# Feed-forward activations with a token's chunks side by side, and one convolution tap of every second chunk moved from VectorE to ScalarE and GpSimd

## The chip, the core and the metric

The kernel runs on one core of a Trainium2 chip. A core has a matrix engine (TensorE, PE in the profile, with its weight loads as PEld), a vector engine (VectorE, DVE), a scalar engine for activations (ScalarE, ACT), a general engine (GpSimd, POOL), and a queue engine that issues most of the transfers (SP). The engines run side by side, each through its own queue in program order, and wait for one another by semaphores. The metric is the device time of the program in microseconds (us), as the median of several runs.

## What is computed

A cross-attention layer followed by a quantized feed-forward layer, each with a residual, for one sequence of 2048 tokens of 256 features and a context of 1601 tokens. The change lies in the feed-forward layer:

```python
def act_quant(x):
    scale = 127.0 / jnp.clip(jnp.max(jnp.abs(x), axis=-1, keepdims=True), 1e-05)
    return jnp.clip(jnp.round(x * scale), -128, 127) / scale
...
h = bit_linear(x, w1)                                        # 256 -> 1024, inputs and weights quantized
h = depthwise_conv1d(h.transpose(0, 2, 1), conv_w, conv_b)   # three taps along the tokens
h = h.transpose(0, 2, 1)
h = jax.nn.silu(h)
return bit_linear(h, w2)                                     # 1024 -> 256, inputs and weights quantized
...
x = x + _L0_xattn_ref(ctx_1024, _layernorm(x, axis=-1), mask_BxS2_bk0, ...)
x = x + _L0_ffn_ref(_layernorm(x, axis=-1), L0_ffn_w1, L0_ffn_conv_w, L0_ffn_conv_b, L0_ffn_w2)
```

The depthwise convolution has for each of the 1024 hidden features its own three weights and a bias: output token t is made of the hidden tokens t-1, t and t+1. The second `bit_linear` quantizes each token's 1024 activations with one scale, which needs the largest magnitude over all of them.

## The kernel before

The attention part comes first: keys and values from the context and the tokens, then eight units (four blocks of 512 query tokens by two pairs of heads), then the output projection, the residual and the quantization of the feed-forward layer's inputs, block of 128 tokens by block. This part ends at about 855 us, but its last four blocks are finished in between the work of the feed-forward part: `plan` holds the calls with the step at which each is due.

The feed-forward part works with features on the 128 partitions and tokens along the free axis. The 1024 hidden features are `NH = 8` chunks of 128. The tokens are taken in 8 groups (`NG`) of `G = 256`. The work is cut into 32 slots: slot s handles group `s // 4` and the pair of chunks `2 * (s % 4)` and the next one (`NP = 4` pairs to a group). `slot(s)` (line 935) writes out the order of the instructions; each engine keeps the program's order, since `tensor`, `vector`, `scalar` and `gpsimd` there are wrappers that forbid reordering (`InOrder`, line 157; the profile puts all of their instructions on line 165, so they are told apart by the names of their tiles). For one pair of chunks the stages are

- `hidden` (line 820): four matmuls with `w1T` into `ph`, 256 tokens and one neighbour on each side, in one of two PSUM buffers. It is called at the end of the slot before.
- `dequantize` (831): DVE multiplies `ph` by the tokens' units `ib_all` into `h`, both chunks in one instruction.
- `taps` (840): ACT makes of `h` the middle tap with the bias, in `t`, and the first tap, in `side`; four instructions of 128x256.
- `last_tap` (854), one slot later: DVE adds the third tap to `t`, one instruction for each chunk; then POOL adds `t` to `side`, both chunks in one instruction.
- `silu` (864), two slots later: ACT puts the Silu of `side` into `t`.

`t` is laid out by chunk and then by token, `[P, NH, G]`. When the four pairs of a group are done, `later_pieces` (928) places, by slots after the group's first:

- 6: `magnitudes` (868), the largest magnitude over the 8 chunks, one DVE reduction of 2048 elements into `m`;
- 7: `columns` and `scales` (875, 881): PE transposes `m`, DVE reduces it over the partitions into `am2` and makes the scale `qsc`; POOL fills `cm` with the scale along rows;
- 8: `scales_spread` (889): PE transposes `cm` into `tpb`, so that each token's scale stands on all partitions; then `rounding(g, 0)`;
- 9: `rounding(g, 1)` (894): DVE multiplies half of `t` (four chunks, all tokens) by the scales and rounds it into `hq`, by adding and taking away a large constant;
- 10: `product` (908): for each of two blocks of 128 tokens eight matmuls, with `hq` as the weights and `w2T` moving, into `py`;
- 11: `residual_out` (918): DVE scales `py`, adds the residual, and SP stores it.

Inside a slot the order is `silu(s-2)`, `dequantize(s)`, `taps(s)`, in slots 3, 7, ... the units of a later group (`unit_rows`, with two `cm` fills on POOL), `last_tap(s-1)`, then the later pieces, and `hidden(s+1)` at the end. So in a slot where a product is due, PE takes the product before the next `ph`.

Of the kernel before, what the change touches and what calls it, by code (L numbers as in the profile page):

```python
# [9 lines left out]
F32 = mybir.dt.float32  # L10
BF16 = mybir.dt.bfloat16
U8 = mybir.dt.uint8
AF = mybir.ActivationFunctionType
ALU = mybir.AluOpType
AX = mybir.AxisListType
PSUM = bass.MemoryType.PSUM

P = 128
FMAX = 3.4028234663852886e38
MAGIC = 12582912.0  # L20
# [6 lines left out]
def kernel(  # L27
# [30 lines left out]
    NH = HID // P  # L58
    NQB = NL // P
    G = 256  # L60
# [45 lines left out]
    w2T = const.tile([P, NH, D], BF16, name="w2T")  # L106
    cw_sb = const.tile([P, NH, 3], F32, name="cw_sb")
# [61 lines left out]
    tensor, vector = InOrder(nc.tensor), InOrder(nc.vector)  # L169
    scalar, gpsimd = InOrder(nc.scalar), InOrder(nc.gpsimd)  # L170
# [36 lines left out]
    with tc.tile_pool(name="pro", bufs=1, side="right") as pro, tc.tile_pool(  # L207
        name="pw", bufs=2, side="right"
# [238 lines left out]
    with att:  # L447
# [297 lines left out]
        for k, (u, j) in enumerate(steps):  # L745
            i = k % NKB
            g, pr = units[u]
# [46 lines left out]
    fp = ctx.enter_context(tc.tile_pool(name="fp", bufs=2))  # L794
# [8 lines left out]
    NP = NH // 2  # L803
    groups_ = [{} for _ in range(NG)]
    chunk = {}
# [32 lines left out]
        chunk[s]["h"] = h  # L838

    def taps(s):  # L840
        g, c = s // NP, s % NP * 2
        if c == 0:
            groups_[g]["t"] = fp.tile([P, NH, G], F32, tag="t", name="t", bufs=3)
        t, h = groups_[g]["t"], chunk[s]["h"]
        side = fp.tile([P, 2, G], F32, tag="side", name="side", bufs=3)
        for j in range(2):
            scalar.activation(
                t[:, c + j, :], h[:, j, 1 : G + 1], AF.Identity,
                bias=cb_sb[:, c + j : c + j + 1], scale=cw_sb[:, c + j, 1:2],
            )  # L850
            scalar.activation(side[:, j, :], h[:, j, 0:G], AF.Copy, scale=cw_sb[:, c + j, 0:1])
        chunk[s]["side"] = side

    def last_tap(s):
        g, c = s // NP, s % NP * 2
        t, h, side = groups_[g]["t"], chunk[s]["h"], chunk[s]["side"]
        for j in range(2):
            vector.scalar_tensor_tensor(
                t[:, c + j, :], h[:, j, 2 : G + 2], cw_sb[:, c + j, 2:3], t[:, c + j, :],
                ALU.mult, ALU.add,  # L860
            )
        gpsimd.tensor_tensor(side, side, t[:, c : c + 2, :], ALU.add)

    def silu(s):
        g, c = s // NP, s % NP * 2
        scalar.activation(groups_[g]["t"][:, c : c + 2, :], chunk.pop(s)["side"], AF.Silu)

    def magnitudes(g):
        b = groups_[g]
        b["m"] = fp.tile([P, G], F32, tag="m", name="m")  # L870
        vector.tensor_reduce(
            b["m"], b["t"].rearrange("p c t -> p t c"), AX.X, ALU.max, apply_absolute_value=True
        )

    def columns(g):
        b = groups_[g]
# [14 lines left out]
        b["tb"] = small("tpb")  # L891
        repeat_rows(b["tb"], b.pop("cm"))

    def rounding(g, c):
        b = groups_[g]
        half = b["t"][:, ts(c, NH // 2), :]
        vector.tensor_tensor(
            half, half,
            b["tb"].rearrange("p i t -> p (i t)").unsqueeze(1).to_broadcast([P, NH // 2, G]),
            ALU.mult,  # L900
        )
        if c == 0:
            b["hq"] = fp.tile([P, NH, G], BF16, tag="hq", name="hq")
        vector.tensor_scalar(
            b["hq"][:, ts(c, NH // 2), :], half, MAGIC, -MAGIC, ALU.add, ALU.add
        )

    def product(g):
        b = groups_[g]
        b["py"] = ps_y.tile([P, QPG, D], F32, tag="py", name="py")  # L910
        for i in range(QPG):
            for c in range(NH):
                tensor.matmul(
                    b["py"][:, i, :], b["hq"][:, c, ts(i, P)], w2T[:, c, :],
                    start=(c == 0), stop=(c == NH - 1),
                )

    def residual_out(g):
# [8 lines left out]

    later_pieces = {
        6: (magnitudes,), 7: (columns, scales),
        8: (scales_spread, lambda g: rounding(g, 0)), 9: (lambda g: rounding(g, 1),),  # L930
        10: (product,), 11: (residual_out,),
    }
    last = NG * NP

    def slot(s):
        if s == 0:
            unit_spread(0)
            unit_spread(1)
            hidden(0)
        if 0 <= s - 2 < last:  # L940
            silu(s - 2)
        if s < last:
            dequantize(s)
            taps(s)
        if s % NP == 3 and s // NP + 2 < NG:
            unit_rows(s // NP + 2)
        if 0 <= s - 1 < last:
            last_tap(s - 1)
        for g in range(NG):
            for call in later_pieces.get(s - g * NP, ()):  # L950
                call(g)
            if g > 1 and s == (g - 2) * NP + 3:
                unit_spread(g)
        if s + 1 < last:
            hidden(s + 1)
# [41 lines left out]
```

## Time and profile before

| | |
|---|---|
| median of 3 runs | 1016.02 us (1014.09 to 1018.25) |
| time of the profiled execution | 1019.8 us, of which the span is 1018.0 us |
| feed-forward part | from about 855 us to the end of the span |
| TensorE clock granted over the span, mean | 0.899; in windows of the feed-forward part 0.56 to 0.63 |
| ACT, taps into `t` and into `side`, 128x256 | 64 each, 0.591 and 0.493 us in the mean |
| ACT, Silu, 128x512 | 32, 0.628 us |
| DVE, third tap, 128x256 | 64, 0.528 us in the mean, 0.476 in the median |
| DVE, maximum over the chunks, 2048 elements to 256 | 8, 3.660 us |
| POOL, `side` plus `t`, 128x512 | 32, 1.270 us |
| PE, product matmuls and their weight loads | 128, 0.421 and 0.151 us in the median |

The profile is of one execution; the sum of the costs is compared with that execution's own time. Instructions of one engine overlap at their ends, so the distance from one start to the next is often somewhat shorter than the duration. A line of the timeline or of the table of groups names the engine, the kernel's line, the operation, the tile written and the tiles read, the shapes, the count, and in the end the idle time of the engine before it with what ended it. In the chain of waits each line is the start, the length, the engine and the tile of one stretch.

### The profile page before, as it was taken

What the parts mean: (1) busy time and instruction counts of PE and PEld (TensorE: products, weight loads), DVE (VectorE), ACT (ScalarE), POOL (GpSimd) and SP (SyncE); (2) the same over time, 40 slices, a digit from 0 to 9 for tenths busy, and PEclk for the clock granted to TensorE, in tenths of its full rate; (3) what the DMA queues carried; (4) which work ended last, traced back from release to release, by engine and by line L of the source; (5) the groups of instructions that cost most, each with busy time, mean ns of one, the idle gap of its engine ahead of it and who ended that gap; (6) DMA issues with size and microseconds to landing.
All of it is one profiled execution on the core that took longest, in us unless ns stands there. A gap on an engine that the chain in (4) does not pass through costs nothing.

```text
span 1018.0 us, 10253 instructions
## 1 busy us (share of the span) xinstructions
PE 859.8 (84%) x3672; PEld 323.7 (32%) x3672; DVE 819.0 (80%) x946; ACT 523.0 (51%) x706; POOL 537.6 (53%) x415
## 2 busy tenths in 40 slices
PE   4788978998998999899899999989998877555543
PEld 3334532222322333232233323223332323333321
DVE  4566447996898689779868998977898995799996
ACT  2456444554654644455454566556554435755560
POOL 2432343556555556646655675646566546545431
PEclk9999998999999999899989999999998897556565
DMA  5010002453444344245534335544344000000000
GB/s 133 21 33 10 1 0 58 87 104 80 86 91 97 83 83 82 62 84 99 109 75 79 75 83 104 96 92 98 69 84 102 22 0 21 1 11 11 21 10 32
DMA packets 29775, 63.28 MB, mean 62 GB/s; under 512 B 7259, under 2 KB 16668, under 8 KB 29724
## 3 DMA queue, kind: packets, MB, share of 16 engines
q0 software_dynamic: 14112, 51.39, 25.8%
q1 hardware_dynamic: 12030, 10.44, 3.3%
q10 hardware_dynamic: 3582, 0.79, 0.4%
q8 instruction: 29, 0.48, 0.2%
q14 instruction: 22, 0.18, 0.1%
HBM read 9.13 MB, written 2.10 MB: 11 GB/s over the span
## 4 chain that ended last, share of the span: by engine, by line
PE 53%; DVE 36%; ACT 5%; issue 2%; POOL 2%; DMA 2%; ACTq 0%; POOLq 0%; DVEq 0%
PE sa L165 15%; PE ot L165 15%; PE st L165 10%; DVE mxs L165 6%; DVE sg L165 5%; PE kv L353 5%; DVE t L165 4%; DVE m L165 3%; PE sa L179 3%; DVE acd L165 2%; DVE y L165 2%; DVE h L165 2%; DVE hi L165 1%; DVE rows L165 1%; DVE hq L165 1%
## 5 line engine op out<-in xcount | busy, mean ns | idle before, releaser
L165 POOL TENSOR_TENSOR acc<-acc,pt 128x1024 f32<-128x1024 f32 x112 | 283.2, 2529 | 36.0 <-ACT pt L165 35.5
L165 PE MATMUL ot<-pt,v_sb 128*64 128x512 f32 x928 | 254.2, 633 | 2.0 <-ACT pt L165 1.9
L165 DVE TENSOR_TENSOR sg<-sg,nb 128x1024 f32<-128x1024 f32 x104 | 218.2, 2104 | 14.1 <-ACT nb L165 14.1
L165 PE MATMUL sa<-q_un,kT 64*128 64x512 f32 x812 | 223.9, 640 | 3.0 <-DVE mxs L165 3.0
L165 POOL DMA_DIRECT2D acd<-pt x98 | 84.0, 857 | 214.6 <-ACT pt L165 156.9
L165 ACT ACTIVATE sg<-sa,maskc 128x1024 f32<-128x1024 f32 x91 | 101.2, 1112 | 177.1 <-PE sa L165 176.9
L165 ACT ACTIVATE pt<-st 128x1024 f32<-128x1024 f32 x128 | 130.9, 1023 | 77.4 <-PE st L165 77.3
L165 DVE TRANSPOSE_TENSOR_REDUCE mxs<-sa 128x32 f32<-128x1024 f32 x112 | 137.2, 1231 | 34.4 <-PE sa L165 33.6
L165 DVE TRANSPOSE_TENSOR_REDUCE mxs<-sg 128x32 f32<-128x1024 f32 x91 | 112.7, 1238 | 40.8 <-ACT sg L165 40.8
L165 PE MATMUL st<-q_un,kT 64*128 64x512 f32 x512 | 141.8, 633 | 0.0
L165 ACT ACTIVATE pt<-sg 128x1024 f32<-128x1024 f32 x104 | 109.3, 1051 | 41.9 <-DVE sg L165 41.9
L165 PEld LDWEIGHTS sa<-q_un,kT 64*128 64x128 f32 x812 | 64.0, 186 | 138.7 <-issue 88.3
L165 PEld LDWEIGHTS ot<-pt,v_sb 128*64 128x64 f32 x928 | 48.8, 139 | 183.8 <-issue 174.1
L165 POOL TENSOR_TENSOR side<-side,t 128x512 f32<-128x512 f32 x32 | 40.6, 1270 | 48.8 <-DVE t L165 47.8
L165 PEld LDWEIGHTS st<-q_un,kT 64*128 64x128 f32 x512 | 53.4, 202 | 34.9 <-issue 31.1
L165 ACT ACTIVATE t<-h,cb_sb,cw_sb 128x256 f32<-128x256 f32 x64 | 37.9, 591 | 38.6 <-DVE h L165 38.6
L353 PE MATMUL kv<-wkv_sb,feat 128*128 128x512 f32 (+1 forms) x116 | 55.5, 620 | 0.0
L165 PE MATMUL st<-rows,ones 64*128 64x512 bf16 x256 | 52.4, 403 | 1.5 <-DVE mxs L165 1.5
L329 DVE TENSOR_TENSOR nn<-raw,ss 128x512 f32<-128x512 f32 (+1 forms) x23 | 15.7, 681 | 47.0 <-POOL ss L101 47.0
L165 PE MATMUL py<-w2T,hq 128*128 128x256 bf16 x128 | 30.2, 417 | 26.4 <-DVE hq L165 26.4
L101 POOL TENSOR_TENSOR ss<-ss,neg_half 128x8 f32<-128x8 f32 (+1 forms) x23 | 37.7, 1638 | 1.9
L97 POOL TENSOR_SCALAR ss<-ss 128x8 f32<-128x8 f32 (+1 forms) x23 | 5.8, 253 | 60.2 <-DVE ss L320 60.1
(130 smaller groups left out, 1001.1 us busy)
## 6 DMA issues: line engine op xcount, KB each, us to landing
acd<-pt POOLq DMA_DIRECT2D x98, 512.0 KB, 4.5
tok<-in_x_dram SPq DMA_DIRECT2D x4, 512.0 KB, 3.5
q_un<-in_x_dram SPq DMA_DIRECT2D x4, 512.0 KB, 3.6
w_sb<-in_L_ffn_w_dram SPq DMA_DIRECT2D x4, 512.0 KB, 3.2
out_dram<-res SPq DMA_DIRECT2D x16, 128.0 KB, 1.8
tok<-in_ctx_dram SPq DMA_DIRECT2D x3, 512.0 KB, 4.1
wkv_sb<-in_L_xattn_W_kv_dram ACTq DMA_DIRECT2D x1, 512.0 KB, 9.0
wo_sb<-in_L_xattn_W_out_dram SPq DMA_DIRECT2D x1, 256.0 KB, 8.8
```

Of the source, the lines that this page charges most:

```text
L97: gpsimd.tensor_scalar(x, x, floor, None, op)
L101: gpsimd.tensor_tensor(x, x, e, ALU.pow)
L165: return tc.keep_in_program_order(getattr(self.engine, name)(*args, **kwargs))
L179: tensor.matmul(st[:, hh, :], kT[halves(hh), pr, ts(j, P)], qT[g][halves(hh), pr, :], start=start, stop=True,)
L329: nc.vector.tensor_tensor(nn[:rows, :nb, :].rearrange("p b (h d) -> p b h d", d=DH), raw[:rows, :nb, :].rearrange("p b (h d) -> p b h d", ...
L353: nc.tensor.matmul(kv[:rows, b, :], feat[:, c, c0 + b * rows : c0 + (b + 1) * rows], wkv_sb[:, c, :], start=(c == 0), stop=(c == ND - 1),)
```

## The change

The sum of the taps is made in new tiles `pre` and `side`, and `t` holds only the result of the Silu, by token and then by chunk, `[P, G, NH]`. ACT's `taps` gets a fifth instruction, the third tap of the second chunk of the pair, in `side[:, 2]`. `last_tap` has one DVE instruction, for the first chunk, instead of two; POOL adds `side[:, 2]` to `side[:, 1]` first (128x256), and then `side` to `pre` (128x512, as before). `silu` writes its two chunks with a step of 8 elements. `magnitudes` reads neighbours. `rounding` takes 128 tokens with all chunks, rather than four chunks with all tokens, and `hq` is by token and then by chunk too, so that the product's weights are read with a step of 8 elements.

```diff
     def taps(s):
-        g, c = s // NP, s % NP * 2
-        if c == 0:
-            groups_[g]["t"] = fp.tile([P, NH, G], F32, tag="t", name="t", bufs=3)
-        t, h = groups_[g]["t"], chunk[s]["h"]
-        side = fp.tile([P, 2, G], F32, tag="side", name="side", bufs=3)
+        c = s % NP * 2
+        h = chunk[s]["h"]
+        pre = fp.tile([P, 2, G], F32, tag="pre", name="pre", bufs=3)
+        side = fp.tile([P, 3, G], F32, tag="side", name="side", bufs=2)
         for j in range(2):
             scalar.activation(
-                t[:, c + j, :], h[:, j, 1 : G + 1], AF.Identity,
+                pre[:, j, :], h[:, j, 1 : G + 1], AF.Identity,
                 bias=cb_sb[:, c + j : c + j + 1], scale=cw_sb[:, c + j, 1:2],
             )
             scalar.activation(side[:, j, :], h[:, j, 0:G], AF.Copy, scale=cw_sb[:, c + j, 0:1])
-        chunk[s]["side"] = side
+        scalar.activation(side[:, 2, :], h[:, 1, 2 : G + 2], AF.Copy, scale=cw_sb[:, c + 1, 2:3])
+        chunk[s].update(pre=pre, side=side)
 
     def last_tap(s):
-        g, c = s // NP, s % NP * 2
-        t, h, side = groups_[g]["t"], chunk[s]["h"], chunk[s]["side"]
-        for j in range(2):
-            vector.scalar_tensor_tensor(
-                t[:, c + j, :], h[:, j, 2 : G + 2], cw_sb[:, c + j, 2:3], t[:, c + j, :],
-                ALU.mult, ALU.add,
-            )
-        gpsimd.tensor_tensor(side, side, t[:, c : c + 2, :], ALU.add)
+        c = s % NP * 2
+        h, pre, side = chunk[s]["h"], chunk[s]["pre"], chunk[s]["side"]
+        gpsimd.tensor_tensor(side[:, 1, :], side[:, 1, :], side[:, 2, :], ALU.add)
+        vector.scalar_tensor_tensor(
+            pre[:, 0, :], h[:, 0, 2 : G + 2], cw_sb[:, c, 2:3], pre[:, 0, :], ALU.mult, ALU.add
+        )
+        gpsimd.tensor_tensor(pre, pre, side[:, 0:2, :], ALU.add)
 
     def silu(s):
         g, c = s // NP, s % NP * 2
-        scalar.activation(groups_[g]["t"][:, c : c + 2, :], chunk.pop(s)["side"], AF.Silu)
+        if c == 0:
+            groups_[g]["t"] = fp.tile([P, G, NH], F32, tag="t", name="t", bufs=3)
+        t = groups_[g]["t"][:, :, c : c + 2]
+        scalar.activation(t.rearrange("p t c -> p c t"), chunk.pop(s)["pre"], AF.Silu)
 
     def magnitudes(g):
...
-        vector.tensor_reduce(
-            b["m"], b["t"].rearrange("p c t -> p t c"), AX.X, ALU.max, apply_absolute_value=True
-        )
+        vector.tensor_reduce(b["m"], b["t"], AX.X, ALU.max, apply_absolute_value=True)
...
-    def rounding(g, c):
+    def rounding(g, i):
         b = groups_[g]
-        half = b["t"][:, ts(c, NH // 2), :]
+        part = b["t"][:, ts(i, P), :]
         vector.tensor_tensor(
-            half, half,
-            b["tb"].rearrange("p i t -> p (i t)").unsqueeze(1).to_broadcast([P, NH // 2, G]),
-            ALU.mult,
+            part, part, b["tb"][:, i, :].unsqueeze(2).to_broadcast([P, P, NH]), ALU.mult
         )
-        if c == 0:
-            b["hq"] = fp.tile([P, NH, G], BF16, tag="hq", name="hq")
-        vector.tensor_scalar(
-            b["hq"][:, ts(c, NH // 2), :], half, MAGIC, -MAGIC, ALU.add, ALU.add
-        )
+        if i == 0:
+            b["hq"] = fp.tile([P, G, NH], BF16, tag="hq", name="hq")
+        vector.tensor_scalar(b["hq"][:, ts(i, P), :], part, MAGIC, -MAGIC, ALU.add, ALU.add)
 
     def product(g):
...
-                    b["py"][:, i, :], b["hq"][:, c, ts(i, P)], w2T[:, c, :],
+                    b["py"][:, i, :], b["hq"][:, ts(i, P), c], w2T[:, c, :],
```

## The prediction

> **What bounds the kernel now.** I read the page first, then the windows of the last 160 us, because every edit lies there, then the chain of waits, the groups of the Vector engine by shape, and the timeline of one period. All times are us.
>
> The page says that TensorE leads over the whole run (DVE is VectorE, ACT ScalarE, POOL GpSimd):
>
> ```profile
> PE 859.8 (84%) x3672; PEld 323.7 (32%) x3672; DVE 819.0 (80%) x946; ACT 523.0 (51%) x706; POOL 537.6 (53%) x415
> ```
>
> The table of windows says otherwise for the feed-forward part (columns: window, length, then busy time and count of PE, PEld, DVE, ACT, POOL, the granted clock, DMA):
>
> ```profile
> 860.00:880.00 20.00, 9.98 (x57) 7.07 (x55) 14.49 (x21) 19.33 (x44) 9.87 (x9) 0.59 0.00 0
> ...
> 920.00:940.00 20.00, 11.43 (x44) 6.53 (x44) 19.59 (x38) 11.24 (x24) 10.26 (x12) 0.57 0.04 13
> ...
> 960.00:980.00 20.00, 10.58 (x47) 5.97 (x47) 18.96 (x35) 13.17 (x28) 10.03 (x11) 0.59 0.08 26
> ```
>
> DVE is busy 19.59 of 20 from about 880 on; only the first 20 us belong to ACT (19.33). The chain of waits, which begins in each period at the maximum over a token's 1024 values, names the same engine:
>
> ```profile
> 935.25 3.58 DVE m L165
> 945.36 1.93 DVE t L165 x3
> 948.75 1.93 DVE t L165 x3
> 954.25 3.57 DVE m L165
> ```
>
> The eight reductions start at 876.8, 896.3, 915.8, 935.2, 954.2, 970.8, 986.9 and 1000.0: periods of 19.5 while blocks of the attention part are still being finished, then 16.7, 16.0 and 13. What DVE does there, by shape:
>
> ```profile
> L165 DVE SCALAR_TENSOR_TENSOR t<-h,cw_sb,t 128x256 f32<-128x256 f32 x64 | 31.5, 528 | 3.2 <-ACT t L165 3.2
> L165 DVE TENSOR_REDUCE m<-t 128x256 f32<-128x2048 f32 x8 | 29.3, 3660 | 0.0
> L165 DVE TENSOR_TENSOR t<-t,tpb 128x1024 f32<-128x1024 f32 x16 | 19.4, 1213 | 4.3 <-PE tpb L165 4.3
> L165 DVE TENSOR_SCALAR hq<-t 128x1024 bf16<-128x1024 f32 x16 | 12.5, 779 | 0.6
> ```
>
> And a stretch of the timeline, for the intervals:
>
> ```profile
> 969.44 0.68 DVE L165 TENSOR_TENSOR h<-ph,ib_all 128x516 f32<-128x516 f32 x1
> 969.58 2.74 PE L165 MATMUL py<-w2T,hq 128*128 128x256 bf16 x12 [2.35 <-DVE hq L165]
> 970.05 0.87 DVE L165 SCALAR_TENSOR_TENSOR t<-h,cw_sb,t 128x256 f32<-128x256 f32 x2
> 970.84 3.66 DVE L165 TENSOR_REDUCE m<-t 128x256 f32<-128x2048 f32 x1
> 971.08 1.27 POOL L165 TENSOR_TENSOR side<-side,t 128x512 f32<-128x512 f32 x1 [2.11 <-DVE t L165]
> 974.42 0.68 DVE L165 TENSOR_TENSOR h<-ph,ib_all 128x516 f32<-128x516 f32 x1
> ```
>
> Successive instructions of one engine overlap a little: two taps end 0.87 after the first began, one alone takes 0.476 (its median), so a second tap is worth 0.39. On ACT a tap into side is followed 0.40 later by the next instruction, one into t 0.49 later, a Silu about 0.52 later.
>
> [...] m, which steps 1024 bytes, costs 3.66 for 2048 elements (1.79 ns each), while w_sb's sums over neighbours take 1.204 for 1024 (1.18 ns each). [...] a tiny 128x2 scaling of am takes 0.17 alone and 1.09 at 960.49, ending just as POOL's add of side (960.29 to 961.55) ends, and taps that meet such an add reach 1.199. [...] The loads of hq take 0.151; no load here is strided.
>
> **The change, part by part.**
>
> *The maximum.* 128x1024 in 1.204 and y's 128x256 in 0.420 give 1.02 ns an element and 0.16 fixed: 2048 neighbours take 2.25. Saved: 8 x (3.66 - 2.25) = 11.3, all on DVE's path, the last in the tail.
>
> *The second tap on DVE.* 32 instructions go, 0.39 each, 12.5 in all. Not all count. The first six stand in the ACT-bound beginning. In the groups with little else (rounding starts at 964.1, 980.2 and 996.2) DVE waits, or comes to wait, for the chain of scale, POOL's cm, transpose: it already idles 0.95 and 1.54 there, and in the group at 958 POOL has two cm, the new add and the old one (1.59 + 0.72 + 1.27) ahead of the next two cm, which end about 6.3 after that slot's h, where DVE now arrives at 6.33. I strike four more. 22 x 0.39 = 8.6.
>
> *The new tap on ACT.* 32 x 0.40 = 12.8. From 880 on ACT is busy 11.2 to 13.2 of 20 and waits for h before each slot of taps (38.6 in all), which hides it. In the beginning nothing hides it: before the first m stand five slots with a fifth tap, 5 x 0.40 = 2.0.
>
> *Silu writing 32 bytes apart.* The trace has no such write. Below: nothing. By DVE's reads: (3.66 - 2.25) / 2048 = 0.69 ns an element, 0.35 for 512. Above: three times that, 1.0. I take 0.35. A slot of ACT then is 1.78 for four taps, 0.40, 0.52 + 0.35 = 3.05, against at least 3.1 on DVE (h 0.61, tap 0.48, rounding 2.0): it just fits. In the beginning four Silu stand before the first m: 4 x 0.35 = 1.4. What helps there: DVE's tap needs only ACT's first instruction of a slot, not the third (0.89 later). The beginning: 2.0 + 1.4 - 0.9 = +2.5.
>
> *POOL.* 32 adds of 128x256, in the row of q_un at least 0.715 each. Per group 4 x (0.72 + 1.27) and two to four cm of 0.6 to 0.8: under 11, against 13 or more; no bound. But the new add waits for ACT alone: it starts when ACT's slot ends, about 3.05 after h, and lasts to 3.8[...]. Before, POOL's only add stood behind that tap and could not meet it. Below: 0; above: 32 x 0.72 = 23. I take 0.1 in half the slots, 1.5.
>
> *Rounding by 128 tokens instead of four chunks.* As many elements, still dense; the scale is now repeated along the innermost axis (step 0). nn, with such an operand, takes 0.693 for 512, a plain h 0.682 for 516, so I price it at nothing[...]. hq keeps its form.
>
> *The product.* Its first token block now needs the first rounding alone, so eight matmuls rather than twelve follow the last rounding: 12 take 2.74, 0.21 apart, four fewer save 0.85 in the tail. Its weights now step 16 bytes[...]: 0.15 to 1.0 a load; I take 0.25[...]. That is 8 x 0.04 = 0.3 in the tail. In the periods the eight, and the four ph matmuls behind them (1.07), must end before the next h: 8 x 0.25 + 1.17 = 3.2 against h, tap and maximum, 0.61 + 0.48 + 2.25 = 3.3. Hidden, barely.
>
> *Buffers.* side goes from three to two; its slot s-2 is free when POOL has added it, which Silu in front of the new taps waits for anyway. t is taken at the Silu instead of the tap. The first writes of the part wait for more earlier loads and additions, all over by 845. Nothing.
>
> Sum: -11.3 - 8.6 + 2.5 + 1.5 - 0.85 + 0.3 = -16.4. The profiled execution, span 1018.0 and time 1019.8, would become 1003.4; the median of the runs is 3.8 below it, so 1016.0 - 16.4 = 999.6, told as 1000.
>
> **The rivals.** *ACT becomes the bound.* Silu's spread writes cost 0.9: the beginning +2.2, and in the short periods a slot is 3.6, 14.8 a group with ib_all, against 13.1: four groups x 1.7 = 7. About -7, 1009. For: ACT has 0.05 to spare in the shortest slots. Against: [...] DVE's price is 0.35.
>
> [...] The new add meets the tap in most slots, 0.35 of 0.72 each on average: 32 x 0.35 = 11 instead of 1.5. -7, again 1009; above 0.65 each it would be no gain. For: am and the taps of 1.199. Against: in slots over 3.4 the add is over before the tap.
>
> *Slower: strided weight loads.* Place: TensorE's queue, where the product stands ahead of the next ph, for which DVE's h waits. Two slots of 3.1 and 3.3 hold 16 loads and 1.17: up to 0.33 a load is hidden (0.27 for the second eight). Beyond, each group waits 16 times the excess; the 16.4 are gone at 0.47, and it is slower by 5 at 0.52. At 0.6 a load: 7 x (9.6 + 1.17 - 6.4) = +31, in sum +14, 1030. For: no strided load has been seen here[...]. Against: 128 elements at DVE's 1.79 ns are 0.23.
>
> **How the numbers follow.** About 0.5% (5 us) is what a measurement of this kernel can tell from no change. Forecast, 0.56; ACT the bound, 0.14; [...] weight loads, 0.17. The forecast's own range: 993 [...] to 1007 [...]. To reach 8 in 10 it takes in most of the first two rivals: 993 to 1013. Faster: all of the forecast, 0.13 of ACT's, [...] 0.75; same 0.07; slower 0.18, nearly all of it the weight loads.
>
> **What would show it.** m at 2.25; 32 taps on DVE at 0.48 and not at 0.8 to 1.2; Silu at about 0.98; hq's loads at about 0.25, with no idle of DVE before h because of ph; the first m about 2.5 later than 876.8, later periods about 16.5 and 13; a last product of eight matmuls. It is wrong if Silu exceeds 1.5, if DVE's taps average above 0.7, or if DVE waits for ph in every group.

## The result, and the profile after

The changed kernel takes 1001.24 us in the median of four runs (998.04 to 1002.59), beside 1016.43 us for the kernel before (four runs, 1014.09 to 1018.25). The ratio is 0.9847, with a 95% interval of 0.9815 to 0.9879: between 12 and 19 us saved, and 15.2 between the two medians. The profiled execution took 1002.59 us with a span of 1000.8, against 1019.8 and 1018.0.

Not all of that difference of 17.2 us between the two spans belongs to the change. The first `h` of the feed-forward part starts at 858.79 before and at 855.70 after, though the attention part ahead of it has the same code in both. Over all the profiled executions below it starts anywhere from 847.3 to 863.5. A second profile of the changed kernel, from a later run, starts it at 852.65 and ends at 997.7. So the shift is a matter of the execution; why the attention part varies was not pursued. What repeats is the stretch from the first `h` to the end: 145.10 in the one profile of the changed kernel and 145.05 in the other. Before it was 159.21. I measure the change by this stretch: **14.1 us saved**. This is where they come from (all times in us, from the starts of `h` and `m` in the traces):

| | before | after |
|---|---|---|
| first `h` to first `m` | 18.02 | 20.28 |
| the seven periods from `m` to `m` | 19.41, 19.48, 19.47, 18.99, 16.68, 16.03, 13.09 | 17.89, 17.33, 17.33, 17.43, 14.79, 13.48, 11.02 |
| their sum | 123.15 | 109.27 |
| last `m` to the end of the span | 18.04 | 15.55 |

The beginning became 2.3 longer, the periods 13.9 shorter, the tail 2.5 shorter. The page's first line, after (engine, busy time, share, instructions):

```profile
PE 859.9 (86%) x3672; PEld 328.0 (33%) x3672; DVE 797.1 (80%) x914; ACT 546.5 (55%) x738; POOL 560.7 (56%) x447
```

DVE lost 22 us of work, ACT and POOL each gained 23. The windows, with the same columns as in the prediction:

```profile
860.00:880.00 20.00, 10.01 (x45) 7.10 (x45) 9.39 (x15) 19.97 (x43) 13.13 (x15) 0.50 0.00 0
...
920.00:940.00 20.00, 12.82 (x54) 7.82 (x53) 19.55 (x36) 16.20 (x32) 14.85 (x18) 0.59 0.04 14
...
960.00:980.00 20.00, 11.22 (x50) 6.81 (x48) 18.54 (x33) 19.50 (x37) 14.13 (x15) 0.67 0.08 27
```

ACT fills the beginning, as before (19.97 of 20). From 920 to 940 DVE is as full as before (19.55), with ACT five us busier. From 960 to 980 ACT reads 19.50, more than DVE; whether it bounds that window is a question for the experiments, not for this line. The chain of waits of the changed kernel (start, length, what) still runs through DVE in a period, and has one new member, `y`:

```profile
911.28 2.20 DVE m L165
...
920.48 1.14 DVE t L165
...
923.45 1.14 DVE t L165
...
925.31 1.29 DVE y L165
...
928.62 2.19 DVE m L165
```

The groups of DVE by shape over the last 150 us (busy time, mean ns of one, idle time before them):

```profile
L165 DVE TENSOR_TENSOR t<-t,tpb 128x1024 f32<-128x1024 f32 x16 | 19.4, 1213 | 4.7 <-PE tpb L165 4.7
L165 DVE TENSOR_REDUCE m<-t 128x256 f32<-128x2048 f32 x8 | 18.2, 2277 | 0.0
L165 DVE SCALAR_TENSOR_TENSOR pre<-h,cw_sb,pre 128x256 f32<-128x256 f32 x32 | 16.6, 519 | 7.3 <-ACT pre L165 7.3
L165 DVE TENSOR_SCALAR hq<-t 128x1024 bf16<-128x1024 f32 x16 | 12.8, 799 | 0.6
...
L165 DVE TENSOR_SCALAR qsc<-qsc 128x2 f32<-128x2 f32 x8 | 5.1, 638 | 0.3
L165 DVE TENSOR_SCALAR y<-q_un,mv 128x256 f32<-128x256 f32 x4 | 4.9, 1234 | 0.0
...
L165 DVE TENSOR_SCALAR am<-am 128x2 f32<-128x2 f32 x8 | 4.5, 557 | 0.3
```

Before, the last three of these read (same view):

```profile
L165 DVE TENSOR_SCALAR am<-am 128x2 f32<-128x2 f32 x8 | 5.9, 732 | 0.3
...
L165 DVE TENSOR_SCALAR y<-q_un,mv 128x256 f32<-128x256 f32 x4 | 1.6, 401 | 0.0
...
L165 DVE TENSOR_SCALAR qsc<-qsc 128x2 f32<-128x2 f32 x8 | 1.4, 170 | 0.3
```

The maximum went from 3.660 to 2.277 and half the taps are gone. But two instructions that the diff doesn't touch grew: `y` from 0.401 to 1.234, and `qsc`, which multiplies two numbers on each partition, from 0.170 to 0.638. Together they take 7.0 more. `am` takes 1.4 less. The timeline shows what runs on POOL beside them (start, length, engine):

```profile
924.61 0.69 DVE L165 TENSOR_SCALAR hq<-t 128x1024 bf16<-128x1024 f32 x1
...
924.81 1.63 POOL L165 TENSOR_TENSOR pre<-pre,side 128x512 f32<-128x512 f32 x1
925.22 1.37 DVE L165 TENSOR_SCALAR y<-q_un,mv 128x256 f32<-128x256 f32 x1
```

```profile
932.97 0.72 POOL L165 TENSOR_TENSOR side<-side 128x256 f32<-128x256 f32 x1
...
933.09 0.63 DVE L165 TENSOR_SCALAR am<-am 128x2 f32<-128x2 f32 x1
...
933.77 1.26 POOL L165 TENSOR_TENSOR pre<-pre,side 128x512 f32<-128x512 f32 x1
...
933.95 1.11 DVE L165 TENSOR_SCALAR qsc<-qsc 128x2 f32<-128x2 f32 x1
```

In the first, POOL's large addition begins while `hq` is running, takes 1.63 instead of about 1.27 and ends at 926.44; `y`, begun in between, ends at 926.59. In the second, `am` runs beside the new small addition, which ends at 933.69, and `qsc` beside the large one, which comes right behind it and ends at 935.03. `y`, `am` and `qsc` each end less than 0.2 after the addition. A timeline shows coincidence, though. The experiments ask whether the additions are the cause.

### The profile page after: what moved, and what is told of

Its sections match the earlier page's. It is cut to its first block, busy times and chain, and to the rows that moved or that the text cites. A ratio compares the mean times of both kernels' runs of the same rounds, so it can differ in the third digit from the quotient of the medians.

```text
span 1000.8 us, 10358 instructions
## 1 busy us (share of the span) xinstructions
PE 859.9 (86%) x3672; PEld 328.0 (33%) x3672; DVE 797.1 (80%) x914; ACT 546.5 (55%) x738; POOL 560.7 (56%) x447
## 4 chain that ended last, share of the span: by engine, by line
PE 55%; DVE 32%; ACT 5%; issue 4%; DMA 2%; POOL 2%; ACTq 0%; POOLq 0%; DVEq 0%
PE sa L165 16%; PE ot L165 16%; PE st L165 10%; DVE mxs L165 5%; DVE sg L165 5%; PE kv L353 5%; PE sa L179 3%; DVE m L165 2%; DVE y L165 2%; DVE acd L165 2%; DVE t L165 2%; DVE h L165 2%; DVE hi L165 1%; DVE rows L165 1%; DVE qsc L165 1%
## 5 line engine op out<-in xcount | busy, mean ns | idle before, releaser
L165 DVE TENSOR_TENSOR sg<-sg,nb 128x1024 f32<-128x1024 f32 x104 | 215.7, 2080 | 13.9 <-ACT nb L165 13.9
L165 POOL TENSOR_TENSOR pre<-pre,side 128x512 f32<-128x512 f32 x32 | 41.8, 1306 | 14.6 <-DVE pre L165 13.3
L165 ACT ACTIVATE side<-h,cw_sb 128x256 f32<-128x256 f32 x96 | 44.4, 494 | 0.0
L165 ACT ACTIVATE pre<-h,cb_sb,cw_sb 128x256 f32<-128x256 f32 x64 | 37.4, 584 | 9.8 <-DVE h L165 9.7
L165 ACT ACTIVATE t<-pre 128x512 f32<-128x512 f32 x32 | 36.5, 1141 | 9.4 <-POOL pre L165 9.4
```

Source lines behind the costliest of these rows:

```text
L165: return tc.keep_in_program_order(getattr(self.engine, name)(*args, **kwargs))
```

## The experiments

Each experiment is an edit of the changed kernel. The expectations use letters: **A**, POOL's new additions hold small instructions of DVE, and this is what the tap's part fell short by; **B**, ACT is what is late now, by Silu's spread writes or by the fifth instruction; and, from the single columns on, **C**, a stall that is removed passes to whatever of DVE's comes next. "Stretch" is first `h` to the end in the profile of that run. Each ratio is to the kernel before, run beside it.

| kernel | stretch | to first `m` | seven periods | tail | median, and ratio to before (95%) |
|---|---|---|---|---|---|
| before | 159.21 | 18.02 | 123.15 | 18.04 | |
| after | 145.10 | 20.28 | 109.27 | 15.55 | 1001.24, 0.9847 (0.9815 to 0.9879) |
| after, once more | 145.05 | 20.29 | 109.29 | 15.47 | 1003.36, 0.9865 (0.9838 to 0.9892) |
| layout alone | 148.17 | 19.12 | 113.55 | 15.50 | 1006.78, 0.9908 (0.9874 to 0.9942) |
| tap alone | 155.84 | 19.19 | 118.91 | 17.74 | 1014.4, 0.9991 (0.997 to 1.0012) |
| Silu dense | 143.69 | 19.18 | 109.08 | 15.43 | 997.72, 0.9833 (0.9797 to 0.9869) |
| without the new addition | 139.84 | 20.30 | 103.84 | 15.70 | 1000.33, 0.9846 (0.9793 to 0.9899) |
| without the fifth tap of ACT | 142.58 | 18.30 | 108.53 | 15.75 | 1000.63, one run |
| large addition later | 144.86 | 20.28 | 108.76 | 15.82 | 1010.22, one run |
| later, six slots on DVE | 143.88 | 19.12 | 108.76 | 16.00 | 1005.47, 0.9897 (0.9864 to 0.9931) |
| the same, chosen slots | 144.96 | 19.12 | 110.31 | 15.53 | 999.81, 0.9883 (0.9806 to 0.9961) |
| Silu by pairs | 144.11 | 19.53 | 109.15 | 15.43 | 1002.15, one run |
| single columns | 143.44 | 20.29 | 107.61 | 15.54 | 998.5, 0.9831 (0.9794 to 0.9868) |
| single columns, six slots on DVE | 142.69 | 19.11 | 107.81 | 15.77 | 999.83, 0.9835 (0.98 to 0.987) |

The medians spread by several us with the start of the feed-forward part, so differences of one to three us are read from the stretch and its parts; the medians decide only the large ones.

**The layout alone.** DVE makes both third taps again, ACT and POOL have nothing new; `t` and `hq` stay by token.

```diff
-        scalar.activation(side[:, 2, :], h[:, 1, 2 : G + 2], AF.Copy, scale=cw_sb[:, c + 1, 2:3])
...
-        gpsimd.tensor_tensor(side[:, 1, :], side[:, 1, :], side[:, 2, :], ALU.add)
-        vector.scalar_tensor_tensor(
-            pre[:, 0, :], h[:, 0, 2 : G + 2], cw_sb[:, c, 2:3], pre[:, 0, :], ALU.mult, ALU.add
-        )
+        for j in range(2):
+            vector.scalar_tensor_tensor(
+                pre[:, j, :], h[:, j, 2 : G + 2], cw_sb[:, c + j, 2:3], pre[:, j, :],
+                ALU.mult, ALU.add,
+            )
```

> The layout alone: both third taps on VectorE as before, Silu, maximum, rounding and product by token and then chunk. From the first h to the end of the span the kernel before took 159.2 us and the changed one 145.1. Theory A [...]: the layout has no new add, so it keeps all of its gain: maximum 8 x 1.38 = 11.0, tail 0.8, less four Silu of 1.13 instead of 0.63 in the beginning, 2.0: 159.2 - 9.8 = 149.4. Theory B (the gain is lost on ScalarE, through Silu's spread writes and the fifth tap): Silu's writes cost outside the beginning as well, about 3: 152.5.

**The tap alone.** `t` and `hq` as before the change, the tap moved.

```diff
-        t = groups_[g]["t"][:, :, c : c + 2]
-        scalar.activation(t.rearrange("p t c -> p c t"), chunk.pop(s)["pre"], AF.Silu)
+        scalar.activation(groups_[g]["t"][:, c : c + 2, :], chunk.pop(s)["pre"], AF.Silu)
...
-        vector.tensor_reduce(b["m"], b["t"], AX.X, ALU.max, apply_absolute_value=True)
+        vector.tensor_reduce(
+            b["m"], b["t"].rearrange("p c t -> p t c"), AX.X, ALU.max, apply_absolute_value=True
+        )
```

(`rounding` and `product` likewise.)

> The moved tap alone, layout by chunk and then token as before. Removed from VectorE: 32 x 0.39 = 12.5, of which the first six are covered and some four more. Theory A (GpSimd's adds hold VectorE): 22 x 0.39 = 8.6, less 2.0 for the fifth taps in the beginning, plus 0.9 for the earlier tap, less 4 held: 159.2 - 3.5 = 155.7 from the first h to the end. Theory B (ScalarE): with dense Silu writes a slot of ScalarE is 2.7 and never the bound, so nothing but the beginning is lost: 159.2 - 7.5 = 151.7.

The layout alone saves 11.0 of the stretch, the tap alone 3.4; together 14.4, beside 14.1 measured with both. The two parts don't lean on one another. Both stretches lie nearer to A's numbers (149.4 and 155.7) than to B's (152.5 and 151.7). In the medians the tap alone can't be told from no change (0.997 to 1.0012). The groups by shape of the layout alone, and below them of the tap alone:

```profile
L165 DVE TENSOR_REDUCE m<-t 128x256 f32<-128x2048 f32 x8 | 18.2, 2278 | 0.0
...
L165 DVE TENSOR_SCALAR y<-q_un,mv 128x256 f32<-128x256 f32 x4 | 1.6, 401 | 0.0
```

```profile
L165 DVE TENSOR_SCALAR qsc<-qsc 128x2 f32<-128x2 f32 x8 | 5.1, 637 | 0.3
L165 DVE TENSOR_SCALAR y<-q_un,mv 128x256 f32<-128x256 f32 x4 | 4.9, 1219 | 0.0
```

The long `y` and `qsc` come with the tap, not with the layout.

**Silu dense.** Silu writes its 512 values side by side into another place of `t`, so that the maximum and the quantization are taken over other values than the reference's; every instruction keeps its size.

```diff
-        t = groups_[g]["t"][:, :, c : c + 2]
-        scalar.activation(t.rearrange("p t c -> p c t"), chunk.pop(s)["pre"], AF.Silu)
+        t = groups_[g]["t"].rearrange("p t c -> p (t c)")[:, c * G : (c + 2) * G]
+        scalar.activation(t.rearrange("p (c t) -> p c t", c=2), chunk.pop(s)["pre"], AF.Silu)
```

> The changed kernel with Silu writing its two chunks densely, into another place of t, so that the maximum and the quantization are taken over other values; every instruction and its size stay. Silu back at 0.63. Theory A (GpSimd's adds hold VectorE): only the beginning gains, 4 x 0.5 = 2.0, and a little at the last groups: 145.1 - 2.5 = 142.6 from the first h to the end. Theory B (ScalarE is the bound again in the last groups): 2.0 and some 1.5 in each of the last three periods: 145.1 - 6.5 = 138.6.

ACT's Silu in the groups, first after, then with this edit:

```profile
L165 ACT ACTIVATE t<-pre 128x512 f32<-128x512 f32 x32 | 36.5, 1141 | 9.4 <-POOL pre L165 9.4
```

```profile
L165 ACT ACTIVATE t<-pre 128x512 f32<-128x512 f32 x32 | 19.9, 623 | 10.5 <-POOL pre L165 10.4
```

The spread writes cost 0.52 each, 16.6 in all. Taking them away gives 1.4 of the stretch: 1.1 before the first `m`, and 0.2 over the seven periods, where B had expected some 1.5 in each of the last three.

**Without the new addition.** POOL doesn't add `side[:, 2]`, so the third tap of every second chunk is left out of the sum; ACT makes it all the same.

```diff
-        gpsimd.tensor_tensor(side[:, 1, :], side[:, 1, :], side[:, 2, :], ALU.add)
```

> The changed kernel without GpSimd's add of the moved tap: ScalarE still makes it, and it is left out of the sum. Theory A (GpSimd's adds hold VectorE's scaling of y, 1.23 us instead of 0.40, and of qsc, 0.64 instead of 0.17): these go back, 3.3 + 3.7 us on VectorE, part of it behind other waits: 145.1 - 5 = 140 from the first h to the end. Theory B (ScalarE): 145.1 - 1 = 144.

```profile
L165 DVE TENSOR_SCALAR am<-am 128x2 f32<-128x2 f32 x8 | 6.0, 754 | 0.3
...
L165 DVE TENSOR_SCALAR y<-q_un,mv 128x256 f32<-128x256 f32 x4 | 1.6, 402 | 0.0
...
L165 DVE TENSOR_SCALAR qsc<-qsc 128x2 f32<-128x2 f32 x8 | 1.4, 170 | 0.3
```

In the groups above `y`, `qsc` and `am` have the durations of the kernel before: 3.3 and 3.7 less than after, `am` 1.6 more, together 5.5; the taps and `hq` change by -0.5 and +0.7. The seven periods shrink by 5.4, the stretch by 5.3. Another reading would be that without the small addition POOL's large one, and with it Silu's input, comes earlier, and that DVE waits less for ACT. The windows of the two stretches, after and then this edit (columns as above), speak against it:

```profile
855.70:1000.80 145.10, 86.03 (x352) 53.95 (x350) 119.92 (x208) 109.77 (x211) 92.82 (x105) 0.58 0.05 15
```

```profile
859.46:999.31 139.85, 80.13 (x352) 50.16 (x350) 114.23 (x208) 108.97 (x211) 67.18 (x73) 0.61 0.05 16
```

DVE executes the same 208 instructions in 5.7 us less of busy time, and stands idle for as long as before (25.2 and 25.6). So the new additions cost 5.3 us of the stretch, and nearly all of it is time by which instructions of DVE that have nothing to do with the tap became longer. The median (1000.33) doesn't show the gain. In the profiled run the first `h` came late (859.46); where it came in the other three is not on record.

**Without the fifth tap of ACT.** POOL's addition stays, with another operand, so that the moved tap is left out and the first chunk's `side` is added in its place.

```diff
-        scalar.activation(side[:, 2, :], h[:, 1, 2 : G + 2], AF.Copy, scale=cw_sb[:, c + 1, 2:3])
...
-        gpsimd.tensor_tensor(side[:, 1, :], side[:, 1, :], side[:, 2, :], ALU.add)
+        gpsimd.tensor_tensor(side[:, 1, :], side[:, 1, :], side[:, 0, :], ALU.add)
```

> The changed kernel without ScalarE's fifth tap: GpSimd's new add stays and adds the first chunk's side instead, so the moved tap is left out of the sum. From the first h to the end of the span the changed kernel took 145.1 us. Theory A (GpSimd's adds hold VectorE's small instructions): only the beginning gains, five times 0.40: 143, with the first maximum 18.3 instead of 20.3 after the first h and the later periods as they are. Theory B (ScalarE): 140, with the later periods shorter by 0.5 each.

The stretch is 2.5 shorter, 2.0 of it before the first `m` and 0.4 in the first period; A had expected 143, B 140. Of the later periods none changes by more than 0.3. With the dense Silu this says what the 19.50 of ACT mean: ACT is nearly full from 960 to 980, and yet taking 0.40 or 0.52 from each of its slots changes the sixth period, which begins there, by 0.3 and 0.2 only.

**The large addition later.** If the large addition holds `y` and `qsc` only because of where it falls, another place for it should help: POOL adds `side` to `pre` after the later pieces of the slot, `cm` fills among them.

```diff
+    def join_taps(s):
+        pre, side = chunk[s]["pre"], chunk[s]["side"]
         gpsimd.tensor_tensor(pre, pre, side[:, 0:2, :], ALU.add)
...
                 call(g)
+        if 0 <= s - 1 < last:
+            join_taps(s - 1)
+        for g in range(NG):
```

> The changed kernel with GpSimd's add of side to pre written behind the later pieces of its slot, so that where a group's scale is due GpSimd fills cm before that add. The same instructions on every engine. Theory A (GpSimd's adds hold VectorE's small instructions): qsc goes back from 0.64 to about 0.17 in the mean, 3.7 us on VectorE's path in the full periods: 145.1 - 3.5 = 141.6 from the first h to the end; y stays at 1.23. Theory B (ScalarE): no change, or a little longer as Silu gets its input later: 145 to 146.

```profile
L165 DVE SCALAR_TENSOR_TENSOR pre<-h,cw_sb,pre 128x256 f32<-128x256 f32 x32 | 19.2, 599 | 7.3 <-ACT pre L165 7.3
...
L165 DVE TENSOR_SCALAR hq<-t 128x1024 bf16<-128x1024 f32 x16 | 14.5, 904 | 0.6
...
L165 DVE TENSOR_SCALAR qsc<-qsc 128x2 f32<-128x2 f32 x8 | 1.4, 170 | 0.3
```

In these groups `qsc` is at 0.170 again, as A said, but almost nothing is gained: the taps take 2.6 more than after and `hq` 1.7 more, and the stretch is 0.24 shorter where A expected 3.5. Most of the stalls moved to other instructions.

**Both taps on DVE where ACT is the bound.** In the first six slots the tap stays on DVE; with the later addition of the edit before.

```diff
+        if s >= 6:
+            scalar.activation(side[:, 2, :], h[:, 1, 2 : G + 2], AF.Copy, scale=cw_sb[:, c + 1, 2:3])
...
+        if s >= 6:
+            gpsimd.tensor_tensor(side[:, 1, :], side[:, 1, :], side[:, 2, :], ALU.add)
+        for j in range(1 if s >= 6 else 2):
```

> The later add of e6_join_later, and both third taps on VectorE, as before the change, in the first six slots, where ScalarE is the bound. Theory A: the first maximum about 1.2 us earlier and qsc as in e6_join_later: 145.1 - 3.5 - 1.2 = 140.4 from the first h to the end. Theory B (ScalarE): 145.1 - 1.2 = 143.9.

The beginning is 1.16 shorter, as in the layout alone (19.12), and the periods don't move: 0.98 of the stretch against the edit before. The 143.88 is the number that B gave (143.9, against A's 140.4), but not for B's reason: A had counted on the gain of the later addition, which the taps took back, 0.610 each in the mean here.

**Chosen slots.** The tap also stays on DVE in the first slot of each group up to slot 20, where `y` is made; the condition is `s >= 6 and (s % NP or s > 20)`.

> As e8_both, and both third taps on VectorE as well for the first pair of chunks of the groups up to the sixth, whose new add stood in front of the add that y meets. Theory A: y goes back from 1.23 to 0.40, 4 x 0.83 = 3.3, against four more taps of 0.39 on VectorE, 1.6: 140.4 - 1.7 = 138.7 from the first h to the end. Theory B (ScalarE): four taps more on VectorE cost 1.6: 145.5.

`y` fell from 1.13 to 0.82, but the periods grew by 1.55 in sum. DVE has four more taps here than in the edit before (ten more than in the changed kernel). Against that edit its taps take 3.1 more, and `y` gave back 1.2. Again the stretch is near B's number (145.5) and far from A's (138.7). (The median is lower than that of the edit before, but the two intervals overlap.)

**Silu by pairs.** The same values into the same places, but in the order token by token, so that two neighbours are written one after the other.

```diff
-        scalar.activation(t.rearrange("p t c -> p c t"), chunk.pop(s)["pre"], AF.Silu)
+        scalar.activation(t, chunk.pop(s)["pre"].rearrange("p c t -> p t c"), AF.Silu)
```

> The changed kernel with Silu running over a token's two chunks first and then over the tokens: [...] the reads step 1024 bytes between two rows of pre. The same elements. [...] if spread reads cost ScalarE what spread writes do, it stays at 1.1 or more. From the first h to the end: 145.1 less about 0.7 for the beginning, or no change.

```profile
L165 ACT ACTIVATE t<-pre 128x512 f32<-128x512 f32 x32 | 23.8, 742 | 10.1 <-POOL pre L165 10.0
```

Silu takes 0.742 in this group instead of 1.141, less than the 1.1 expected with spread reads, and less than the 0.88 that half of the extra price would leave (0.623 + 0.52 / 2), although it now reads alternately from two places 1024 bytes apart. The stretch is 1.0 shorter, 0.75 of it in the beginning.

**Single columns.** If it is their two elements that make `am` and `qsc` wait, one element at a time should not. In the function that makes the scales, `n` is 2 for a group and 1 for a block of tokens of the attention part, so that only the scalings of the groups change:

```diff
-        vector.tensor_scalar(amax, amax, QUANT_EPS, None, ALU.max)
+        for i in range(n):
+            vector.tensor_scalar(amax[:, i : i + 1], amax[:, i : i + 1], QUANT_EPS, None, ALU.max)
...
-        vector.tensor_scalar(sc[:, :n], sc[:, :n], 127.0, None, ALU.mult)
+        for i in range(n):
+            vector.tensor_scalar(sc[:, i : i + 1], sc[:, i : i + 1], 127.0, None, ALU.mult)
```

> The changed kernel with the two scalings of a group's scale made on one column at a time (128x1, twice) instead of 128x2. In the profiles so far no 128x1 scaling was ever long (0.15 us), while those of 128x2 were 0.56 (am) and 0.64 (qsc) in the mean. Theory A[...]: am and qsc go back to 0.15 each, twice, and the stalls go: 9.6 us of am and qsc become 4.8, 145.1 - 4 = 141 from the first h to the end. Theory C (the stalls are a share of GpSimd's busy time and go to whatever of VectorE's comes next, as in e6_join_later): at most 1 less, 144, with hq or the taps longer instead. Theory B (ScalarE): 145.

The groups, first `y` times `qsc` after, then three groups with this edit, and the timeline at one place:

```profile
L165 DVE TENSOR_SCALAR y<-y,qsc 128x256 f32<-128x256 f32 x4 | 1.4, 342 | 0.0
```

```profile
L165 DVE TENSOR_SCALAR y<-y,qsc 128x256 f32<-128x256 f32 x4 | 5.6, 1390 | 0.0
...
L165 DVE TENSOR_SCALAR qsc<-qsc 128x1 f32<-128x1 f32 x20 | 2.3, 150 | 0.4
...
L165 DVE TENSOR_SCALAR am<-am 128x1 f32<-128x1 f32 x16 | 1.7, 149 | 0.3
```

```profile
909.13 0.73 POOL L165 TENSOR_TENSOR side<-side 128x256 f32<-128x256 f32 x1
...
909.25 0.22 DVE L165 TENSOR_SCALAR am<-am 128x1 f32<-128x1 f32 x2
...
909.70 0.21 DVE L165 TENSOR_SCALAR qsc<-qsc 128x1 f32<-128x1 f32 x2
...
909.94 1.26 POOL L165 TENSOR_TENSOR pre<-pre,side 128x512 f32<-128x512 f32 x1
909.96 1.39 DVE L165 TENSOR_SCALAR y<-y,qsc 128x256 f32<-128x256 f32 x1
```

Twice as many instructions take less than half the time. With the four `qsc` of the token blocks, which were single already, `am` and `qsc` were busy for 10.2 after, and for 4.0 here. At the place shown they aren't held: the small addition runs on POOL from 909.13 to 909.86, and the two `am` that begin during it take 0.22 together, the two `qsc` 0.21. The means of 0.149 and 0.150 leave no room for a wait like the 1.1 of `qsc` after. But soon after them `y` times `qsc` starts 0.02 behind the large addition and lasts until 0.15 after its end: 1.390 instead of 0.342, 4.2 in all. Of the 6.2 gained 1.7 are left in the stretch. Theory C is right, and it doesn't contradict A: the addition is the cause, and which instruction pays depends on the order in which they come.

**Single columns, with both taps on DVE in the first six slots** (without the later addition):

> The single columns of e11_split, and both third taps on VectorE in the first six slots. Theory A: 141 - 1.2 = 139.8 from the first h to the end, about 5 us below the changed kernel in time. Theory C: 144 - 1.2 = 142.8, 2 us below it.

**The changed kernel once more**, beside it on the same chip:

> The changed kernel itself once more, on the same chip as e12_best, to compare the two: 145.1 us from the first h to the end, as in its first profile, if that stretch is the same in each execution, while what stands before it differs by some us from one to the next.

The stretch is 142.69, as C had it (142.8), against 145.05: 1.2 less in the beginning, 1.5 less in the periods, 0.3 lost in the tail. It is the shortest of all versions that compute the whole sum. The medians, 999.83 and 1003.36, lie in that order, but the intervals of their ratios overlap, so that it beats the changed kernel is shown for the stretch and not for the median. Silu by pairs on top of it was not tried.

## Why the prediction was right, point by point

The predicted -16.4 stands beside -14.1 of the stretch and -15.2 of the medians; the profiled difference of 17.2 holds 3.1 that aren't the change's. The forecast case came, and the mechanism with it: the maximum carries most of the gain, DVE stays the bound in the periods, and ACT and POOL hide most of their added work. But the sum is nearer than its terms. The new addition cost 3.9 more than predicted, while the taps and the tail gave 1.7 more; that these errors went against one another was luck, and so was part of the nearness of the medians (1001.24, told as 1000), which hold whatever the attention part did in those executions. The full periods show it: predicted at about 16.5, they are 17.3 to 17.9, and 16.1 to 16.7 without the new addition.

- *The maximum*, -11.3. Measured 2.277 instead of 3.660, eight times 1.383 is -11.1, and the layout alone shortens each period by 1.37 in the mean. Right, and all of it on the path. The way to the number was to take the price of dense reading from other lines of the same engine. POOL's additions don't lengthen it here: seven of the eight ran beside one and one beside none, and all lie between 2.272 and 2.280.
- *The beginning*, +2.5. Measured +2.26. Its parts, by difference: from the changed kernel the spread writes are worth 1.1 there, by the dense Silu, and the fifth tap 2.0; less about 0.8 for the help of DVE's earlier tap. Predicted 1.4, 2.0 and -0.9.
- *Silu's spread write*, taken as 0.35 between nothing and 1.0. It is 0.52 (1.141 against 0.623 dense). Half as much again as predicted, and it made only 0.2 of difference over the seven periods, since ACT's slots had to last longer than DVE's to matter. The rival "ACT becomes the bound" needed 0.9.
- *The taps off DVE*, -8.6, and *POOL's addition*, +1.5. These are the mis-sized terms. From the layout alone to both, the periods lose 4.3, where the two terms say 7.1. Without the new addition they lose 9.7. So the taps are worth about 25 times 0.39 rather than 22 times, and the addition costs 5.4, not 1.5. The step that failed was where the collision was looked for. The prediction set the new addition, which it had end 3.8 after `h` in the shortest slots, against DVE's tap of the same chunk, which it had begin there at about 3.7. That collision is there, but small: five of the 32 taps run beside the new addition for 0.56 to 0.68 instead of 0.476, which is 0.7 in all. Most of the cost stands in the scalings of the scales and of `y`, where the prediction had seen one such wait (the `am` of 1.09) and priced none. How the two engines come to hold one another was not shown by any run. For the three taps more there is a likely reason: in the layout alone three of the second taps within the periods take 0.95 to 0.96 instead of 0.476, and these three are among the taps that go: 1.4 in all. The kernel before has three such taps too, and POOL's addition to `q_un` runs beside each of them (0.87 or 0.88 long). The rival in which the new addition meets the tap in most slots put the cost at 11, twice the 5.4, and in the same wrong place; by its own terms there would have been no gain from 0.56 an addition on ((16.4 + 1.5) / 32), not from 0.65.
- *The tail*, -0.85 + 0.3. Measured -2.5 from the last `m`, of which the maximum itself is 1.4. The rest is -1.1. Eight loads and not twelve follow the last `hq`, and DVE waits 2.02 for `py`, where before it waited 2.83. The end of the timeline before, and of the changed kernel:

```profile
1010.41 0.69 DVE L165 TENSOR_SCALAR hq<-t 128x1024 bf16<-128x1024 f32 x1
1011.15 2.26 PEld L165 LDWEIGHTS <-hq 128*128 128x128 bf16 x12 [1.30 <-DVE hq L165]
...
1013.93 0.88 DVE L165 SCALAR_TENSOR_TENSOR res<-py,am,q_un 128x256 f32<-128x256 f32 x2 [2.83 <-PE py L165]
```

```profile
993.18 1.47 PEld L165 LDWEIGHTS <-hq 128*128 128x128 bf16 x8 [2.34 <-DVE hq L165]
...
994.29 0.69 DVE L165 TENSOR_SCALAR hq<-t 128x1024 bf16<-128x1024 f32 x1
995.04 1.47 PEld L165 LDWEIGHTS <-hq 128*128 128x128 bf16 x8 [0.39 <-DVE hq L165]
997.01 0.88 DVE L165 SCALAR_TENSOR_TENSOR res<-py,am,q_un 128x256 f32<-128x256 f32 x2 [2.02 <-PE py L165]
```

- *The strided weight loads*, 0.25. They take 0.163 in the mean and 0.165 in the median, against 0.140 and 0.151 before. The groups before and after:

```profile
L165 PEld LDWEIGHTS <-hq 128*128 128x128 bf16 x128 | 16.5, 140 | 39.8 <-DVE hq L165 33.7
```

```profile
L165 PEld LDWEIGHTS <-hq 128*128 128x128 bf16 x128 | 19.2, 163 | 25.8 <-DVE hq L165 21.6
```

  The rival that ended on the slower side needed 0.47 for no gain; 0.02 more a load is hidden, and DVE's idle time before `h` because of `ph` is 9.5 in both profiles. The prediction had added 0.10, which was the author's assumption; the only measured number near its 0.25 was the 0.23 that 128 elements take at DVE's 1.79 ns. The runs show 0.02.
- *Rounding with a scale of step 0*, nothing. 1.213 before and after.

## What to carry to other kernels

Work taken from the engine that bounds and given to another one can come back in part, when the other engine's new instructions make the first engine's instructions longer: here 5.4 us of the 9.7 that the taps were worth in the periods. Look for it in instructions that the edit doesn't name, above all tiny ones with a mean several times their minimum (`qsc`: 0.638 in the mean, 0.170 alone). Moving the other engine's work in time, or mending the instruction that pays, mostly passed the stall on to the next one here: with the later addition `qsc` gave back 3.7 and the stretch 0.24, with the single columns `am` and `qsc` gave back 6.2 and the stretch 1.7. The change of layout, which turned the bounding engine's strided read into a dense one, was worth three times as much as the moved tap (11.0 against 3.4), for a price that fell, outside the beginning, on engines with spare time.

## What the runs showed of the hardware that was not expected

- A DVE `tensor_scalar` of 128x2 (`am` or `qsc`), 0.170 alone, lasted until 0.02 to 0.03 after the end of POOL's addition each time that it began during one (11 times in the profile after, up to 1.19). Of 128x1 it took 0.149 to 0.150 in the mean, and two of them begun during an addition took 0.22 together.
- The order of its writes made much of the price of ACT's Silu here: 128x512 took 0.623 when it wrote its values densely, 0.742 when it wrote them two by two with 32 bytes from pair to pair, and 1.141 when each was written 32 bytes from the last. With the 0.742 it also read alternately from two places 1024 bytes apart; which part of the 0.12 over the dense form is due to the reads was not separated.
- The loads of `hq` as weights (128x128 bf16) took 0.163 with a step of 16 bytes, against 0.140 without it, in the mean (medians 0.165 and 0.151).
